# Where the column sums' products stand, and when an image's last output is finished: a fused attention kernel in fp32 pieces

## The chip, the cores and the metric

The kernel runs on one core of a Trainium2 chip. The metric is the device time of one execution in microseconds; the time before is a median of three runs, 2464.89 us (2459.27 to 2466.72). All profile lines are from one profiled execution.

## The reference, cut to what matters

```python
q = einsum('bwhc,cd->bwhd', x, Wq) + bq      # x: 4 images, 64 x 64 x 256
k = einsum('bwhc,cd->bwhd', x, Wk) + bk      # 128 channels
v = einsum('bwhc,cd->bwhd', x, Wv) + bv      # 256 channels
pq, pk, pv = (t.reshape(B, -1, 4096) for t in (q, k, v))
energy = einsum('bcn,bcm->bnm', pq, pk)      # 4096 x 4096 for each image
attention = softmax(energy, axis=-1)
out = einsum('bcm,bnm->bcn', pv, attention)
return gamma * out.reshape(x.shape) + x
```

For each image it is an attention over 4096 positions with 128 channels for q and k and 256 for v. The softmax is not shifted by its maximum on the main path: the kernel takes the exponential directly, sums it over m, and divides at the end.

## The kernel before, in words

**Stages.** The four images (`b`) run one after the other, and the order of every instruction on every engine is written out by hand. Each image has two stages.

*Projection*, 16 steps `i`. A step transposes an x tile on TensorE (`xt`, L123), copies it out of PSUM on ScalarE (`xts`, L129), and multiplies for q and k (`qk`, L136) and for v (`v`, L157). VectorE and ScalarE split q and k into fp32r pieces `f` (L259, L261), and POOL's queue stores these in DRAM (`kf`, L264; `qd`, L266). The x tiles are loaded by SP's queue (L82) into three buffers, so a load waits until the transposes of three tiles before are done. v is split into `vh`, `vl`, `vd` (L279, L283); the last two v tiles are split later, in units 2 and 6 of the attention.

*Attention*, 128 units `u` of 256 rows of m each. Sixteen units make a group `g` of 512 columns n; an image has eight groups. A unit does, in this order on TensorE: two "cross" products for the unit three ahead (L308), the first half's six products (`attend(b, u, 0)`, L365: two with `vh` and two with `vl` into bank a0, two with `vd` into b0), four energy products for the unit two ahead (L323), and the second half's six products (a1, b1). ScalarE scales the cross products in place (L309), takes the exponentials (L326) and their upper pieces `h` (L332). VectorE adds the exponentials into the running sum `s` (L341) and makes the lower pieces `ld` (L346, L348). POOL's queue loads k (L296), three units ahead of their use in the energies, and q (L290).

**PSUM.** Four banks (`ps_e`) hold energies, and four (`ps_o`) hold the results of a group: a0, b0, a1, b1. A tile that takes a bank waits until the bank's former tile has been read. At the end of a group `emptied` (L379) reads a0 and b0 after the first half of unit 15, and a1 and b1 after its second half, all on ScalarE.

**The finish of a group.** In unit 15 the running sum is split into two pieces `zf` (L388, L390). `finish` is a generator: `start` runs it up to its first `yield`, and each `proceed` runs it one `yield` on. Its pieces are:

1. two products of ones with the pieces of the sum (`z`, L400, in a bank of `ps_o`) and a copy of one row of the result by ScalarE (L401);
2. the store of that row in DRAM (`zd`, L403, SP);
3. its load, spread over partitions (`rall`, L405, SP);
4. the reciprocal (L407) and the addition of the a and b parts of the output (L408), on VectorE;
5. the store of the reciprocals (`rd`, L410, SP);
6. their load, broadcast to all partitions (`r`, L413, SP);
7. after one empty piece, the multiplication of the output by r (L416, VectorE);
8. the load of x that adds to the output in SBUF (L420, POOL's queue);
9. after one empty piece, the store of the output (L423, SP).

`proceed` is called once in each unit that doesn't end a group. It is also called in every projection step, and once between images. So an image's last group, started at the end of unit 127, is finished in the projection of the next image. Between images TensorE does the z products, the transposes of the next image's second tile (`transposed(1)`) and the qk products of its first (`project_qk(b + 1, 0)`). The last group of the last image has a path of its own, `finish_last`.

SP's and POOL's queues issue their transfers in the order of the program: a transfer that waits for its data holds those behind it.

Of the kernel before, what the change touches and what calls it, by code (L numbers as in the profile page):

```python
# [9 lines left out]
F32 = mybir.dt.float32  # L10
# [10 lines left out]
def kernel(  # L21
# [36 lines left out]
    nc = tc.nc  # L58
    B, W, H, C = x.shape
    P = 128  # L60
# [26 lines left out]
    ones_r = const.tile([P, P], F32R, name="ones")  # L87
# [86 lines left out]
    NB = 512  # L174
    NJ = NB // P
    NG = N // NB
# [22 lines left out]
    with ExitStack() as fast:  # L199
# [10 lines left out]
        ps_o = pool("ps_o", 1, space=PSUM)  # L210
# [9 lines left out]
        images, qd, kf, units, loads, now = [], {}, {}, {}, {}, {}  # L220
# [9 lines left out]
        def proceed():  # L230
            for pieces in list(active):
                if next(pieces, StopIteration) is StopIteration:
                    active.remove(pieces)
# [20 lines left out]
        def project_qk(b, i):  # L254
            images[b].qk(i)
            qk = now["qk"]
            f = ppool.tile([P, 2, 2, 3, P], F32R, tag="ld", name=f"f_{b}_{i}")
            h = f[:, :, :, 0, :]
            nc.scalar.activation(h, qk, AF.Identity, scale=UPPER / 64)  # L259
            for j, s, op in ((1, -64.0, ALU.add), (2, 64.0 * (1.0 + E), ALU.subtract)):  # L260
                nc.vector.scalar_tensor_tensor(  # L261
                    f[:, :, :, j, :], h.bitcast(F32), s, qk, ALU.mult, op
                )
            nc.gpsimd.dma_start(kf[b, i], f[:, 1])  # L264
            for s in range(2):
                nc.gpsimd.dma_start(qd[b, i // NJ + NG // 2 * s][:, i % NJ], f[:, 0, s])  # L266
# [21 lines left out]
        def load_q(b, g):  # L288
            t = work.tile([P, NJ, 3, P], F32R, tag="q", name=f"q_{b}_{g}")
            nc.gpsimd.dma_start(t, qd[b, g])  # L290
            loads[b, "q", g] = t
# [7 lines left out]
        def forms(b, u, i, f):  # L299
            return loads[b, "k", u][:, i, f, :], loads[b, "q", u // NU][:, :, f, :]  # L300
# [10 lines left out]
        def energy(b, u):  # L311

            if u >= STEPS:
                return
            if u % NU:
                x = ppool.tile([P, 2, NB], F32, tag="x", name=f"x_{b}_{u}", bufs=3)
            else:
                x = ppool.tile([P, 2, NB], F32, tag="s", name=f"s_{b}_{u // NU}")
            units[b, u] = x
            for i in range(2):  # L320
                e = units.pop((b, "e", u, i))
                for f in range(2):
                    nc.tensor.matmul(  # L323
                        e, *forms(b, u, i, f), start=False, stop=(f == 1), skip_group_check=True
                    )
                nc.scalar.activation(x[:, i, :], e, AF.Exp, scale=(1.0 + E) / E)  # L326
# [47 lines left out]
        def emptied(b, g, j):  # L374

            if j == 0:
                now["o"] = work.tile([P, 2, 2, NB], F32, tag="o", name=f"o_{b}_{g}", bufs=1)
            for c, scale in enumerate((gam1, gam)):
                nc.scalar.activation(  # L379
                    now["o"][:, c, j, :], now["ab"[c], j], AF.Identity, scale=scale  # L380
                )

        def sum_forms(b, g):
# [6 lines left out]
            nc.vector.tensor_tensor(l, s[:, 0, :], h.bitcast(F32), ALU.subtract)  # L390
            yield

        def finish(b, g, o, s):
            n = b * NG + g
            r4 = rall[:, n, :]
            row = lambda t: t[n : n + 1, :]
            spread = lambda t: row(t).rearrange("o (p j) -> (o p) j", j=NJ)
            zp = ps_o.tile([P, NB], F32, tag="b0", name=f"z_{b}_{g}")
            for f, x in enumerate(now["z"]):
                nc.tensor.matmul(zp, ones_r, x, start=(f == 0), stop=(f == 1))  # L400
            nc.scalar.copy(s[0:1, 0, :], zp[0:1, :])  # L401
            yield
            nc.sync.dma_start(row(zd), s[0:1, 0, :])  # L403
            yield
            nc.sync.dma_start(r4, spread(zd))  # L405
            yield
            nc.vector.reciprocal(r4, r4)  # L407
            nc.vector.tensor_tensor(o[:, 0], o[:, 0], o[:, 1], ALU.add)  # L408
            yield
            nc.sync.dma_start(spread(rd), r4)  # L410
            yield
            r = work.tile([P, NB], F32, tag="r", name=f"r_{b}_{g}", bufs=1)
            nc.sync.dma_start(r, rd[n, :].partition_broadcast(P))  # L413
            yield
            yield
            nc.vector.tensor_tensor(  # L416
                o[:, 0], o[:, 0], r.unsqueeze(1).to_broadcast([P, 2, NB]), ALU.mult
            )
            yield
            nc.gpsimd.dma_start(o[:, 0], xg[b, g], accum_op=ALU.add)  # L420
            yield
            yield
            nc.sync.dma_start(og[b, g], o[:, 0])  # L423
# [49 lines left out]
        def begin(b, i):  # L473

            if i in (4, 5, 6, 7):
                load_k(b, i - 4)
            if i == 6:
                load_q(b, 0)
            if i in (11, 13):
                energy(b, (i - 11) // 2)  # L480
            if i in (10, 11, 13):
                cross(b, (i - 9) // 2)
            if i == 12:
                load_k(b, 4)
            if i in (12, 14):
                upper(b, i // 2 - 6)

        image(0)
        for b in range(B):
            pr = images[b]  # L490
            if b == 0:
                now["banks"] = energies
                pr.transposed(0)

                wp = ps_o.tile([P, P], F32, tag="b1", name="wp1")
                for _ in range(2):
                    nc.tensor.matmul(wp, ones, ones, start=True, stop=True)
                pr.transposed(1)
                project_qk(b, 0)
            for i in range(1, NI):  # L500
                if i == 3:
                    now["banks"] = outputs
                if i + 1 < NI:
                    pr.transposed(i + 1)
                begin(b, i)
                project_qk(b, i)
                if i == NI - 1:
                    halves(b, 0)
                project_v(b, i - 1)
                proceed()  # L510
            project_v(b, NI - 1)
            for u in range(STEPS):
                g, t = divmod(u, NU)
                final = (b, u) == (B - 1, STEPS - 1)
                if t == 6 and g + 1 < NG:
                    load_q(b, g + 1)
                if u == STEPS - NU and b + 1 < B:
                    image(b + 1)
                if u >= STEPS - 3 and b + 1 < B:
                    now["banks"] = energies  # L520
                    if u == STEPS - 3:
                        images[b + 1].load(0)
                    elif u == STEPS - 2:
                        images[b + 1].transposed(0)
                if (b, u) == (B - 1, STEPS - 6):
                    xr = ppool.tile([P, 2, NB], F32, tag="s", name="xr")
                    nc.sync.dma_start(xr, xg[b, g])

                beside = iter(())
                if u in (2, 6):  # L530
                    beside = halve_v(b, NI - 2 + u // 4)
                cross(b, u + LOOK + 1)
                if t == NU - 1 and not final:
                    total = now["sum"]
                    for _ in sum_forms(b, g):
                        pass
                if not final:
                    attend(b, u, 0)
                    if t == NU - 1:
                        emptied(b, g, 0)  # L540
                energy(b, u + LOOK)
                next(beside, None)
                upper(b, u + LOOK)
                load_k(b, u + LOOK + 3)
                halves(b, u + 1)
                next(beside, None)
                if final:
                    finish_last(b, u, xr)
                    break
                attend(b, u, 1)  # L550
                if t == NU - 1:
                    emptied(b, g, 1)
                    start(finish(b, g, now["o"], total))
                else:
                    proceed()
            if b + 1 < B:
                images[b + 1].transposed(1)
                project_qk(b + 1, 0)
                proceed()

    NB = 512
    NG = N // NB
    NJ = NB // P
    NP = NM // 2
    with tc.If(nc.values_load(again[0:1, 0:1]) > 0), ExitStack() as general:
# [7 lines left out]
        ps_o = pool("go", 1, space=PSUM)  # L573
        for b in range(B):
# [16 lines left out]
            for g in range(NG):  # L591
                ps = []
                mx = work.tile([P, 2, NB], F32, tag="mx", name=f"gmx_{b}_{g}")
                for t in range(NP):
                    sp = ps_s.tile([P, 2, NB], F32, tag="s", name=f"gs_{b}_{g}_{t}")
                    for h in range(2):
# [4 lines left out]
                            start=True,  # L601
                            stop=True,
# [31 lines left out]
                for t, p in enumerate(ps):  # L634
# [8 lines left out]
                    for h in range(2):  # L643
                        for s in range(2):
# [4 lines left out]
                                start=(t == h == 0),  # L649
                                stop=(2 * t + h == NM - 1),  # L650
# [43 lines left out]
```

## Time and profile before

| what | before |
|---|---|
| median of three runs | 2464.89 us (2459.27 to 2466.72) |
| the profiled execution | 2466.14 us, span 2464.4 us |
| granted TensorE clock, mean of the span | 0.991 |
| busy TensorE / VectorE / ScalarE | 97% / 84% / 75% |
| SP waits for the copy of z (L403 <- L401) | 1231.0 us, 31 times |
| SP waits for the accumulating load (L423) | 639.4 us, 31 times |
| mean DMA rate | 137 GB/s |

A row of the timeline gives the start in us, the duration in us, the engine, the line, the operation, what it writes and reads, the sizes, the count of merged instructions, and in brackets how long the engine stood idle before it and what ended that. PE is TensorE, DVE VectorE, ACT ScalarE; a q behind an engine's name stands for its queue. A row of the waits gives the waiting engine and line, what ended the wait, and then the total in us, the number of times and the longest. A row of windows gives the two ends and the width, the busy time of PE, PEld (weight loads), DVE, ACT and POOL with their counts, the granted clock, the DMA engines' busy share and GB/s. A row of DMA issues gives the count, the size of each and the median time from issue to landing in us. TensorE's products are pipelined: one of 512 columns is shown with 0.39 us, but the next starts 0.23 us after it.

### The profile page before, as it was taken

To read this page: it belongs to the slowest core of one execution; us is meant where nothing else is said; L and a number is where in the kernel's file an instruction comes from. 1 tells how busy PE (TensorE), PEld (TensorE's weight loads), DVE (VectorE), ACT (ScalarE), POOL (GpSimd) and SP (SyncE) were. 2 spreads that over 40 slices of the span, in tenths; PEclk is the share of its full clock that TensorE was granted. 3 is DMA by queue.
4 is the path that set the end of the run, shared out by engine and by line. 5 is a ranking of instruction groups with operands and counts; after the bars stand their busy time and mean duration, and the time that the engine had idled before them with its cause. 6 is when DMAs were issued, how large, how long until landed. Compare 5 with 4: busy or idle time off the path is not lost.

```text
span 2464.4 us, 30518 instructions
## 1 busy us (share of the span) xinstructions
PE 2391.0 (97%) x10588; PEld 1973.5 (80%) x10588; DVE 2072.6 (84%) x2058; ACT 1856.3 (75%) x3071; POOL 429.3 (17%) x781
## 2 busy tenths in 40 slices
PE   9999999999899999999989999999998999999998
PEld 7888888888788888888867888888887788888886
DVE  5888888888688888888868888888886988888887
ACT  5777777787577877877757777777875787787775
POOL 4211111110321111111032111111113111111110
PEclk9999999999999999999999999999999999999999
DMA  8544444444854444444484444444449444444443
GB/s 257 155 122 118 129 113 127 129 127 101 258 148 129 114 125 126 121 122 131 105 258 146 125 122 122 123 119 122 129 110 269 135 130 125 122 122 125 117 121 90
DMA packets 155215, 338.22 MB, mean 137 GB/s; under 512 B 23471, under 2 KB 56751, under 8 KB 155054
## 3 DMA queue, kind: packets, MB, share of 16 engines
q0 software_dynamic: 114656, 293.52, 44.0%
q1 hardware_dynamic: 39854, 42.41, 5.7%
q8 instruction: 87, 1.43, 0.2%
q14 instruction: 74, 0.61, 0.1%
q10 hardware_dynamic: 544, 0.26, 0.0%
HBM read 268.89 MB, written 67.24 MB: 136 GB/s over the span
## 4 chain that ended last, share of the span: by engine, by line
PE 80%; ACT 11%; DMA 4%; DVE 2%; issue 1%; POOL 0%; SPq 0%; ACTq 0%; DVEq 0%; POOLq 0%
PE a L365 33%; PE b L365 18%; PE e L323 17%; PE e L308 8%; DMA qd<-f 3%; ACT o L379 3%; ACT h L332 2%; PE qk L136 2%; ACT s L326 1%; ACT x L326 1%; PE v L157 1%; DMA x<-in_x_dram 1%; ACT e L309 1%; ACT v L166 1%; ACT f L259 1%
## 5 line engine op out<-in xcount | busy, mean ns | idle before, releaser
L326 ACT ACTIVATE x<-e 128x512 f32<-128x512 f32 x960 | 522.3, 597 | 408.9 <-PE e L323 408.9
L341 DVE TENSOR_TENSOR s<-s,x 128x1024 f32<-128x1024 f32 x480 | 587.8, 1225 | 182.7 <-ACT x L326 174.1
L365 PE MATMUL b<-ld,vd 128*128 128x512 f32 x2048 | 634.6, 391 | 27.1 <-ACT s L401 24.4
L365 PE MATMUL a<-ld,vl 128*128 128x512 f32 x2048 | 631.8, 390 | 3.9 <-DVE ld L346 3.9
L365 PE MATMUL a<-h,vh 128*128 128x512 f32 x2048 | 632.1, 390 | 0.5 <-ACT v L166 0.5
L346 DVE TENSOR_TENSOR ld<-x,h 128x1024 fp32r<-128x1024 f32 x480 | 585.4, 1220 | 3.9 <-DMA qd<-f 3.9
L348 DVE SCALAR_TENSOR_TENSOR ld<-h,x 128x1024 fp32r<-128x1024 f32 x480 | 585.2, 1219 | 0.0
L296 POOL DMA_DIRECT2D k<-kf x512 | 272.4, 532 | 1702.4 <-PE e L323 1569.2
L323 PE MATMUL e<-q,k 128*128 128x512 f32 x2048 | 551.5, 391 | 0.0
L309 ACT ACTIVATE e<-e 128x512 f32<-128x512 f32 x1024 | 543.9, 564 | 0.0
L332 ACT ACTIVATE h<-x 128x1024 fp32r<-128x1024 f32 x480 | 509.6, 1062 | 14.9
L365 PEld LDWEIGHTS b<-ld,vd 128*128 128x128 f32 x2048 | 381.5, 188 | 119.6 <-ACT s L401 36.6
L365 PEld LDWEIGHTS a<-ld,vl 128*128 128x128 f32 x2048 | 384.4, 188 | 85.6 <-DVE ld L346 5.6
L323 PEld LDWEIGHTS e<-q,k 128*128 128x128 f32 x2048 | 385.4, 189 | 80.4
L365 PEld LDWEIGHTS a<-h,vh 128*128 128x128 f32 x2048 | 384.2, 188 | 81.8 <-ACT v L166 1.0
L308 PE MATMUL e<-q,k 128*128 128x512 f32 x1024 | 318.0, 392 | 0.0
L308 PEld LDWEIGHTS e<-q,k 128*128 128x128 f32 x1024 | 192.8, 189 | 40.0
L261 DVE SCALAR_TENSOR_TENSOR f<-f,qks 128x512 fp32r<-128x512 f32 x128 | 82.8, 689 | 60.4 <-ACT f L259 60.4
L136 PE MATMUL qk<-wqk_sb,xts 128*128 128x256 f32 x512 | 127.2, 393 | 0.6 <-ACT xts L129 0.5
L259 ACT ACTIVATE f<-qks 128x512 fp32r<-128x512 f32 x64 | 40.4, 630 | 110.6 <-DVE qks L145 73.8
L157 PE MATMUL v<-xts,wv_sb 128*128 128x256 f32 x512 | 121.7, 382 | 1.2 <-DVE qks L145 1.2
L157 PEld LDWEIGHTS v<-xts,wv_sb 128*128 128x128 f32 x512 | 98.3, 192 | 15.7 <-PE qk L136 2.0
(68 smaller groups left out, 1044.8 us busy)
## 6 DMA issues: line engine op xcount, KB each, us to landing
k<-kf POOLq DMA_DIRECT2D x512, 384.0 KB, 3.4
kf<-f POOLq DMA_DIRECT2D x64, 384.0 KB, 3.3
qd<-f POOLq DMA_DIRECT2D x128, 192.0 KB, 3.6
q<-qd POOLq DMA_DIRECT2D x32, 768.0 KB, 5.0
x<-in_x_dram SPq DMA_DIRECT2D x64, 256.0 KB, 5.3
o<-in_x_dram POOLq DMA_DIRECT2D x31, 512.0 KB, 5.9
out_dram<-o SPq DMA_DIRECT2D x31, 512.0 KB, 3.6
r<-rd SPq DMA_DIRECT2D x31, 256.0 KB, 4.1
```

The source lines that it names most:

```text
L136: nc.tensor.matmul(qk[:, s, :], self.xt[i][:, k, s, :], wqk_sb[:, k, :], start=(k == 0), stop=(k == KC - 1),)
L157: nc.tensor.matmul(vp[:, eh, :], wv_sb[:, k, eh * P : (eh + 1) * P], self.xt[i][:, k].rearrange("p s a -> p (s a)"), start=(k == 0), stop= ...
L296: nc.gpsimd.dma_start(t, kf[b, u % NU])
L308: nc.tensor.matmul(e, *forms(b, u, i, 2), start=True, stop=False, skip_group_check=True)
L309: nc.scalar.mul(e, e, -1.0 / (1.0 + E))
L323: nc.tensor.matmul(e, *forms(b, u, i, f), start=False, stop=(f == 1), skip_group_check=True)
L326: nc.scalar.activation(x[:, i, :], e, AF.Exp, scale=(1.0 + E) / E)
L332: nc.scalar.activation(h, units[b, u], AF.Identity, scale=UPPER)
L341: nc.vector.tensor_tensor(s, s, x, ALU.add)
L346: nc.vector.tensor_tensor(l, x, h.bitcast(F32), ALU.subtract)
L348: nc.vector.scalar_tensor_tensor(d, h.bitcast(F32), 1.0 + E, x, ALU.mult, ALU.subtract)
L365: nc.tensor.matmul(to, (vh, vl, vd)[f][:, t + NU * i, j * P : (j + 1) * P], units[b, u][f][:, i, :], start=(t == 0 and i == 0 and f != 1), ...
```

## The change

The z products and the copy leave `finish` and become a function of their own, `sums`. z takes bank b1 in place of b0. Inside an image `sums` is called for group g - 1 in unit 0 of group g, behind the first half's products and ahead of the energies. At an image's end it is called between the transposes and the qk products of the next image. The two other calls of `proceed`, in the projection's steps and between images, are gone, so the finish of an image's last group goes on in units 0 to 9 of the next image's first group. `start` now runs `finish` up to a `yield` ahead of the store of zd.

```diff
+        def sums(b, g, s):
+            zp = ps_o.tile([P, NB], F32, tag="b1", name=f"z_{b}_{g}")
+            for f, x in enumerate(now["z"]):
+                nc.tensor.matmul(zp, ones_r, x, start=(f == 0), stop=(f == 1))
+            nc.scalar.copy(s[0:1, 0, :], zp[0:1, :])
+
         def finish(b, g, o, s):
...
-            zp = ps_o.tile([P, NB], F32, tag="b0", name=f"z_{b}_{g}")
-            for f, x in enumerate(now["z"]):
-                nc.tensor.matmul(zp, ones_r, x, start=(f == 0), stop=(f == 1))
-            nc.scalar.copy(s[0:1, 0, :], zp[0:1, :])
             yield
             nc.sync.dma_start(row(zd), s[0:1, 0, :])
...
                 project_v(b, i - 1)
-                proceed()
             project_v(b, NI - 1)
...
                     attend(b, u, 0)
                     if t == NU - 1:
                         emptied(b, g, 0)
+                    elif t == 0 and g:
+                        sums(b, g - 1, total)
                 energy(b, u + LOOK)
...
             if b + 1 < B:
                 images[b + 1].transposed(1)
+                sums(b, NG - 1, total)
                 project_qk(b + 1, 0)
-                proceed()
```

## The prediction

> **What bounds the kernel now.** I read the page first, then TensorE's waits, then the timeline at the places where they lie.
>
> ```profile
> span 2464.4 us, 30518 instructions
> PE 2391.0 (97%) x10588; PEld 1973.5 (80%) x10588; DVE 2072.6 (84%) x2058; ACT 1856.3 (75%) x3071; POOL 429.3 (17%) x781
> ```
>
> TensorE sets the time: all other engines have room, so a microsecond counts where TensorE stands still. Its waits (total, times, longest):
>
> ```profile
> PE b L365 <- ACT s L401: 24.4, 28, 0.9
> PE xt L123 <- DMA x<-in_x_dram: 21.7, 8, 7.2
> ```
>
> Both belong to the change. The first comes at each of the 28 passages from one group to the next inside an image (4 images, 8 groups, 7 passages each); the second lies in the projections. A passage in the timeline:
>
> ```profile
> 145.65 1.22 DVE L348 SCALAR_TENSOR_TENSOR ld<-h,s 128x1024 fp32r<-128x1024 f32 x1
> 145.87 0.62 PE L400 MATMUL z<-zf,ones 128*128 128x512 f32 x2
> 147.26 0.62 PE L365 MATMUL a<-ld,vl 128*128 128x512 f32 x2
> 147.57 0.68 ACT L379 ACTIVATE o<-b,gam 128x512 f32<-128x512 f32 x1
> 148.14 0.56 ACT L401 COPY s<-z 1x512 f32<-1x512 f32 x1
> 148.61 1.04 ACT L309 ACTIVATE e<-e 128x512 f32<-128x512 f32 x2
> 148.75 0.72 PE L365 MATMUL b<-ld,vd 128*128 128x512 f32 x2 [0.87 <-ACT s L401]
> 149.99 1.09 ACT L326 ACTIVATE x<-e 128x512 f32<-128x512 f32 x2 [0.33 <-PE e L323]
> ```
>
> z takes bank b0. The next group's b products need b0 and wait until the copy of z is done, and the copy stands on ACT behind the emptying of a1 and b1. From 145.87 to 147.26 TensorE issues six products, 0.23 us apart; with the two at 147.26 the ninth slot is 147.72. It starts at 148.75, so a passage loses 1.03 us.
>
> The projections, by the v products of images 0, 1, 2 and 3 (min/median/max ns, first and last start):
>
> ```profile
> L157 PE MATMUL v<-xts,wv_sb x128: 379/379/634, 12.6 to 77.7; 128*128 128x256 f32 x128
> ```
> ```profile
> L157 PE MATMUL v<-xts,wv_sb x128: 379/379/631, 616.6 to 691.8; 128*128 128x256 f32 x128
> ```
> ```profile
> L157 PE MATMUL v<-xts,wv_sb x128: 379/379/454, 1230.7 to 1306.0; 128*128 128x256 f32 x128
> ```
> ```profile
> L157 PE MATMUL v<-xts,wv_sb x128: 379/379/379, 1844.9 to 1916.9; 128*128 128x256 f32 x128
> ```
>
> The same 128 products take 65.1 us in image 0 and 75.2, 75.3 and 72.0 us after it. Image 0 has no earlier group to finish, and the one wait of its projection is not for x:
>
> ```profile
> PE xt L123 <- ACT v L166: 1.9, 1, 1.9
> ```
>
> What the finish does to image 1:
>
> ```profile
> 659.80 0.59 SPq L423 DMA_DIRECT2D out_dram<-o  x1
> 660.48 7.48 SPq L82 DMA_DIRECT2D x<-in_x_dram  x4
> 666.30 1.09 PE L123 MATMUL xt<-ident,x 128*128 128x128 f32 x4 [5.67 <-DMA x<-in_x_dram]
> 669.75 2.45 PE L136 MATMUL qk<-wqk_sb,xts 128*128 128x256 f32 x8
> ```
>
> SP issues in program order. The store L423 waits for the accumulating load to land, and the next x loads stand behind it: they go out at 660.48, and TensorE idles 5.67 us until 666.30. The load of r (L413, which waits for rd) stands ahead of x loads in the same way. Behind the long wait eight qk products take 2.45 us; elsewhere 1.89 (row at 612.70 below).
>
> **The change, part by part.**
>
> *z in the next group's first unit, in b1 (28 times).* No instruction is added; two products and a copy move. From 145.87 on TensorE now does the two crosses, four a and two b products, with z ninth. The b products come up at 147.26 instead of 147.72; their ld is ready at 145.65 + 1.22 = 146.87, 0.39 us earlier, so no new wait. z needs b1, whose emptying ends at 147.57 + 0.68 = 148.25; with the 0.05 us that lie between the copy's end (148.70) and the product it released (148.75), z starts at 148.30. The wait does not vanish, it changes its owner and shrinks from 1.03 to 0.58 us: 0.45 us a passage, **12.6 us** in all. Behind the waiting z on TensorE stand four energy products and then the second half's a and b. The scalings L309 move ahead of the copy, so they start 0.47 us sooner; the copy follows at about 149.1, ends at 149.7, and the second half's b products come up at 148.30 + 10 x 0.23 = 150.6, 0.9 us later: covered. The exponentials start at about 149.7 instead of 149.99. Bounds: no gain, if the copy slips behind both exponentials (1.09 us against that 0.9); 1.03 us each (28.8 us) if b1 were free in time.
>
> *No proceed in the projections (3 images).* The zd, rall, rd, r and out transfers leave SP's queue ahead of the x loads; the accumulating load leaves POOL's queue between the stores of kf and qd; a reciprocal, an addition and a multiplication leave VectorE. What is then left is what image 0 has, so I take its 65.1 us: 10.1 + 10.2 + 6.9 = **27.2 us**. It isn't the floor: image 0 itself waits 1.9 us for ACT and slows behind it. Bounds: below, that only the bytes matter:
>
> ```profile
> o<-in_x_dram POOLq DMA_DIRECT2D x31, 512.0 KB, 5.9
> out_dram<-o SPq DMA_DIRECT2D x31, 512.0 KB, 3.6
> r<-rd SPq DMA_DIRECT2D x31, 256.0 KB, 4.1
> ```
> ```profile
> 616.50:692.00 75.50, 65.48 (x309) 55.90 (x308) 50.35 (x93) 42.79 (x85) 28.10 (x52) 0.93 0.83 250
> 147.00:214.00 67.00, 66.13 (x292) 54.37 (x291) 58.23 (x53) 53.09 (x88) 10.17 (x18) 1.00 0.48 126
> ```
>
> 1.25 MB at the 250 GB/s of image 1's window are 5.2 us an image, 16 in all. Above, TensorE's own work: busy 65.48 us in that window, partly at a clock of 0.93, so about 60.9 at full clock; 4.2 below image 0's 65.1, so 12.6 more over three images, 39.8 in all.
>
> The clock shows in these windows as 0.93 with the long waits and 1.00 across the 1 us waits of the passages. The Trainium skill (TensorE: Matmul & The Clock Gate, "HAM oscillation — how this bites in real kernels") says that gaps over some 3.4 us drop the array to half its clock until it has been busy again. The trace agrees as far as the 2.45 against 1.89 us go. By that rule at most 1.7 us a long gap would come back, which image 0's time already counts.
>
> *z at an image's end (3 images).* It now stands behind the four transposes and ahead of qk:
>
> ```profile
> 611.79 0.63 PE L400 MATMUL z<-zf,ones 128*128 128x512 f32 x2
> 612.12 0.68 ACT L379 ACTIVATE o<-b,gam 128x512 f32<-128x512 f32 x1
> ...
> 612.26 0.60 PE L123 MATMUL xt<-ident,x 128*128 128x128 f32 x4
> ...
> 612.70 1.89 PE L136 MATMUL qk<-wqk_sb,xts 128*128 128x256 f32 x8
> ```
>
> The transposes now start at 611.79 and end issuing at 612.23; z waits for b1 until 612.80 + 0.05 and takes 0.46, so qk starts at 613.31, not 612.70: 0.6 us an image, **1.8 us lost** (0, if a later wait swallows it).
>
> *The finish in the next image's first group (3 images).* Group 0 also splits the last two v tiles on VectorE in units 2 and 6, the very units in which the finish adds and multiplies. Group 0 of image 1, then the finish in group 1:
>
> ```profile
> 710.43 1.22 DVE L348 SCALAR_TENSOR_TENSOR ld<-h,x 128x1024 fp32r<-128x1024 f32 x1
> 712.37 0.62 PE L365 MATMUL b<-ld,vd 128*128 128x512 f32 x2
> 723.27 0.69 DVE L283 SCALAR_TENSOR_TENSOR vl<-vh,v 128x512 fp32r<-128x512 f32 x1 [1.10 <-ACT vh L279]
> 726.75 1.22 DVE L348 SCALAR_TENSOR_TENSOR ld<-h,x 128x1024 fp32r<-128x1024 f32 x1
> 728.69 0.62 PE L365 MATMUL b<-ld,vd 128*128 128x512 f32 x2
> ```
> ```profile
> 763.97 0.34 SPq L405 DMA_DIRECT2D rall<-zd  x1
> ```
> ```profile
> 772.71 0.17 DVE L407 RECIPROCAL rall<-rall 128x4 f32<-128x4 f32 x1
> 773.91 1.22 DVE L341 TENSOR_TENSOR s<-s,x 128x1024 f32<-128x1024 f32 x1
> ...
> 789.03 1.22 DVE L416 TENSOR_TENSOR o<-o,r 128x1024 f32<-128x1024 f32 x1
> 790.16 1.22 DVE L341 TENSOR_TENSOR s<-s,x 128x1024 f32<-128x1024 f32 x1
> ```
>
> Reciprocal and addition hold VectorE 773.91 - 772.71 = 1.20 us, the multiplication 1.13. The tile ready at 711.65 is needed at 712.37: 0.72 spare, so 0.48 late. In unit 6 VectorE first waits 1.10 us for ACT, which absorbs the older delay; then 727.97 + 1.13 against 728.69 is 0.41 late. Together 0.9 us an image, **2.7 us lost** (bounds 0 and 2.33 us an image). The SP and POOL issues cost nothing here: SP has no x loads then, and POOL's k loads run three units ahead, as in 28 other groups. The images' outputs come later, but the last image's end is untouched.
>
> Sum: -12.6 - 27.2 + 1.8 + 2.7 = -35.3 us. The profiled execution took 2466.14 us (1.7 outside its span), so 2430.8; the median shown is 2464.89, and on it the forecast is **2429.6 us**.
>
> **The rivals.**
>
> *Bytes, not order.* The Trainium skill (DMA: Bandwidth & Descriptors, "Issuing engines are not separate DMA queues") says that transfers of all issuing engines share the same 16 DMA engines and interleave, which speaks against gaining much by reordering queues. As a mechanism here: the x loads are late for want of bandwidth, and the projections gain only the 16 us above: 2464.89 - 24 = 2441. For it: the DMA share of 0.83 in the window above. Against it: image 0 loads and stores the same x, qd and kf without a wait for x, and the x loads of 660.48 weren't even issued before.
>
> *Projections near TensorE's floor.* The relief also ends the ACT waits: 39.8 us, 2417. Against it: image 0 has them without any finish.
>
> *The passage keeps its wait.* The copy slips behind the exponentials, or z's wait is as long as the old one: 12.6 us fewer, 2442. For it: only 0.39 and 0.9 us of margin.
>
> *Slower.* VectorE, in order, is held at the reciprocal in group 0 because the zd and rall transfers queue behind the projection's last stores. In group 1 the reciprocal runs 8.7 us after rall's issue at 763.97, so it costs from a return over 8.7 us on. To eat the whole gain it must hold TensorE another 38 / 3 = 12.7 us an image; at 17 us an image the time would be 2478. Against it: even r, of 256 KB, lands in 4.1 us.
>
> **How the numbers follow.** Forecast 0.66; bytes 0.12; floor 0.08; passage 0.09; slower mechanism 0.05, of which 0.03 end beyond 0.3% and 0.02 within it. A measurement of this kernel tells 0.3% (7.4 us) from no change. So faster 0.94, same 0.03 (0.01 for two shortfalls at once), slower 0.03. The range, 2416 to 2444, reaches to the floor, bytes and passage cases.
>
> **What would show it.** A wait of z for ACT o, 28 times, about 0.4 us as the page counts it, in place of 24.4 us; passages 0.45 us nearer; the v rows of images 1 to 3 at about 65 us, with no SP store between x loads and almost no xt wait for x; in group 0 of images 1 to 3 two new short waits for ld L348. I am wrong if the v rows stay above 70 us, or if the wait at z is 1 us.

## The result, and the profile after

The changed kernel takes 2434.12 us in the median of four runs (2433.08 to 2438.69), beside 2463.74 us for the kernel before: a ratio of 0.9885, 95% interval 0.9865 to 0.9905. That is 29.6 us less where 35.3 were forecast, and inside the range. The profiled execution took 2433.35 us, 32.8 less than that of before. The page's first lines:

```profile
span 2431.6 us, 30522 instructions
PE 2385.8 (98%) x10588; PEld 1963.4 (81%) x10588; DVE 2071.1 (85%) x2058; ACT 1851.9 (76%) x3071; POOL 429.2 (18%) x781
```

TensorE's waits (total, times, longest):

```profile
PE z L396 <- ACT o L379: 11.8, 31, 0.5
PE xt L123 <- ACT v L166: 8.4, 4, 2.9
...
PE a L365 <- DVE ld L346: 4.8, 4, 1.8
PE b L365 <- DVE ld L348: 4.1, 12, 0.5
```

The wait of b for the copy (24.4 us) is gone, and so is that of xt for x (21.7 us). z has a wait of its own, for ScalarE's emptying of b1. In the projections xt now waits for ScalarE. The first passage in the timeline, and the z of the next one:

```profile
147.03 0.62 PE L365 MATMUL b<-ld,vd 128*128 128x512 f32 x2
147.28 0.68 ACT L379 ACTIVATE o<-b,gam 128x512 f32<-128x512 f32 x1
147.84 1.08 ACT L309 ACTIVATE e<-e 128x512 f32<-128x512 f32 x2
148.01 0.73 PE L396 MATMUL z<-zf,ones 128*128 128x512 f32 x2 [0.36 <-ACT o L379]
148.57 1.09 PE L323 MATMUL e<-q,k 128*128 128x512 f32 x4
148.83 0.58 ACT L397 COPY s<-z 1x512 f32<-1x512 f32 x1
149.31 1.06 ACT L326 ACTIVATE x<-e 128x512 f32<-128x512 f32 x2
...
150.40 0.62 PE L365 MATMUL b<-ld,vd 128*128 128x512 f32 x2
...
214.48 0.73 PE L396 MATMUL z<-zf,ones 128*128 128x512 f32 x2 [0.38 <-ACT o L379]
```

z's slot is 147.03 + 0.46 = 147.49. ScalarE frees b1 at 147.28 + 0.68 = 147.96, and z starts at 148.01, 0.52 us late. From one z to the next it is 214.48 - 148.01 = 66.47 us. Before, it was from 145.87 to this:

```profile
212.83 0.62 PE L400 MATMUL z<-zf,ones 128*128 128x512 f32 x2
```

That is 66.96 us: a group with its passage is 0.49 us shorter. The v products of images 1, 2 and 3 after the change:

```profile
L157 PE MATMUL v<-xts,wv_sb x128: 379/379/379, 1218.5 to 1283.0; 128*128 128x256 f32 x128
```
```profile
L157 PE MATMUL v<-xts,wv_sb x128: 379/379/631, 613.7 to 680.9; 128*128 128x256 f32 x128
...
L157 PE MATMUL v<-xts,wv_sb x128: 379/379/379, 1820.5 to 1886.6; 128*128 128x256 f32 x128
```

In image 1 they span 67.2 us, in image 2 (the row that stands alone) 64.5, in image 3 66.1; before 75.2, 75.3 and 72.0. In image 1 SP now issues its x loads with nothing between them, and stores zd only behind the last of them, at 658.81; but ScalarE waits:

```profile
640.48 18.28 SPq L82 DMA_DIRECT2D x<-in_x_dram  x4
...
649.80 0.63 ACT L259 ACTIVATE f<-qks 128x512 fp32r<-128x512 f32 x1 [5.11 <-DMA qd<-f]
651.21 0.66 PE L123 MATMUL xt<-ident,x 128*128 128x128 f32 x4 [2.75 <-ACT v L166]
652.34 3.26 PE L136 MATMUL qk<-wqk_sb,xts 128*128 128x256 f32 x8
...
658.81 0.46 SPq L405 DMA_DIRECT2D zd<-s  x1
```

The next tile of f needs a buffer whose stores to qd haven't landed; ScalarE, in order, holds the evacuation of v behind it, and TensorE stops. It is the kind of wait that image 0 had before.

The two profiled executions, cut at the starts of named TensorE products:

| stretch | before, us | after, us | difference |
|---|---|---|---|
| last b product of an image to the next image's first v, three times | 15.1 | 17.3 | +2.2 |
| v products, images 1 to 3 | 222.4 | 197.7 | -24.7 |
| first group, images 1 to 3 | 204.7 | 207.3 | +2.6 |
| groups 1 to 7 of all images | 1859.4 | 1847.7 | -11.7 |
| image 0 up to its group 1 | 146.1 | 145.4 | -0.7 |
| what is left | 16.6 | 16.2 | -0.4 |

The z of the passage out of group 0 (0.46 us) stood in the first group's stretch before and stands in the next now. With that put right, 28 passages gained 13.5 us, 0.48 each, and the first groups of images 1 to 3 lost 3.9 us, not 2.6.

The windows of the v products after the change, of image 1 and then of image 2:

```profile
613.50:681.00 67.50, 64.12 (x309) 54.53 (x307) 47.86 (x89) 42.22 (x85) 26.89 (x51) 0.97 0.86 256
1218.50:1283.50 65.00, 62.57 (x309) 53.24 (x307) 47.92 (x90) 42.05 (x85) 26.93 (x51) 1.00 0.89 268
```

Before, image 1's window was 75.50 us with TensorE busy for 65.48, at a clock of 0.93. So of its 8.0 us, 6.6 are idle time that is gone, and 1.4 are products, which run at a lower clock for less of the time.

### The profile page after: what moved, and what is told of

Same layout as the page of the kernel before. It is cut to its first block, busy times and chain, and to the rows that moved or that the text cites. A ratio compares the mean times of both kernels' runs of the same rounds, so it can differ in the third digit from the quotient of the medians.

```text
span 2431.6 us, 30522 instructions
## 1 busy us (share of the span) xinstructions
PE 2385.8 (98%) x10588; PEld 1963.4 (81%) x10588; DVE 2071.1 (85%) x2058; ACT 1851.9 (76%) x3071; POOL 429.2 (18%) x781
## 4 chain that ended last, share of the span: by engine, by line
PE 80%; ACT 11%; DMA 4%; DVE 2%; issue 2%; POOL 0%; ACTq 0%; DVEq 0%; POOLq 0%
PE a L365 34%; PE e L323 17%; PE b L365 17%; PE e L308 8%; DMA qd<-f 4%; ACT o L379 3%; ACT h L332 2%; ACT s L326 1%; PE qk L136 1%; ACT x L326 1%; PE z L396 1%; PE v L157 1%; ACT v L166 1%; ACT f L259 1%; ACT e L309 1%
## 5 line engine op out<-in xcount | busy, mean ns | idle before, releaser
L136 PEld LDWEIGHTS qk<-wqk_sb,xts 128*128 128x128 f32 x512 | 95.0, 193 | 17.7 <-ACT xts L129 5.2
```

The lines of the kernel that those rows point to most:

```text
L136: nc.tensor.matmul(qk[:, s, :], self.xt[i][:, k, s, :], wqk_sb[:, k, :], start=(k == 0), stop=(k == KC - 1),)
```

## The experiments

Times are medians, beside runs of the kernel before on the same chip. "v products" are the spans of images 1, 2 and 3 from the first to the last start. A single execution differs from the median by up to 7 us, so the terms are read from the traces.

**One half each.** First, only the z of the passages moves; an image's last group keeps the old course:

```diff
 # against the changed kernel
         def finish(b, g, o, s):
+            if g == NG - 1:
+                zp = ps_o.tile([P, NB], F32, tag="b0", ...)   # products and copy as before
...
                 project_v(b, i - 1)
+                proceed()
...
-                sums(b, NG - 1, total)
                 project_qk(b + 1, 0)
+                proceed()
```

> Only the z products inside an image move (unit 0 of the next group, bank b1); an image's last group keeps its z in b0 and its finish in the next projection. Theory (the passage and the projection are separate terms): the 28 passages lose 0.5 us instead of 1.0 and nothing else changes, about -13.4 us against before, some 2450; the v products of images 1 to 3 stay at 72 to 75 us. Rival (the terms hang together, the gain in the passages being a shift of VectorE's or ScalarE's lateness): passages gain less than 8 us here, or the projections move too.

Measured: 2449.32 us beside 2464.48, ratio 0.9936 (0.992 to 0.9953): 15.2 us less by the medians, 15.8 by the ratio. Its waits:

```profile
PE xt L123 <- DMA x<-in_x_dram: 25.7, 10, 6.5
PE z L396 <- ACT o L379: 10.4, 28, 0.4
```

The passages are those of the changed kernel. The v products stay at 73.9, 75.6 and 74.5 us. So the passages' gain stands by itself.

Second, only the two calls of `proceed` go:

```diff
 # against the kernel before
                 project_v(b, i - 1)
-                proceed()
...
                 project_qk(b + 1, 0)
-                proceed()
```

> Only the finish of an image's last group waits for the next attention; z stays in b0 in its old place. Theory: v products of images 1 to 3 at 64 to 67 us as in the changed kernel (together about 25 us less than before), 0.9 us an image lost in group 0, passages at 1.0 us as before: about -22 us, some 2442. Rival (the projections gained from the new place of z as well): v products stay above 70 us in at least one image.

Measured: 2445.34 us beside 2464.48, ratio 0.9915 (0.9899 to 0.993): 19.1 us less by the medians, 21 by the ratio.

```profile
PE b L365 <- ACT s L401: 24.4, 28, 0.9
PE xt L123 <- ACT v L166: 11.9, 4, 4.7
PE a L365 <- DVE ld L346: 7.6, 4, 4.0
...
PE xt L123 <- DMA x<-in_x_dram: 0.8, 1, 0.8
```

The wait for x is gone but for 0.8 us, and the v products take 69.6, 64.5 and 64.4 us, while the passages' 24.4 us stand as before. The first product that needs a lower piece in a first group waits longer here, up to 4.0 us, and that in image 0, which the edit doesn't touch.

**Order or bytes.** In the kernel before, ScalarE's queue issues the x loads of images 1 to 3, a step further ahead; the finish stays in the projection with all its bytes:

```diff
 # against the kernel before
-                self.xs[g] = load_x(self.xpool, self.b, g)
+                self.xs[g] = load_x(self.xpool, self.b, g, nc.scalar if self.b and g > 2 else nc.sync)
...
-            for g in range(i, i + 2):
+            for g in range(i, i + (3 if self.b else 2)):
                 self.load(g)
```

> The kernel before, but the x loads of images 1 to 3 from the fourth on are issued by ScalarE's queue, one step further ahead, so that they no longer stand behind the finish on SP. The finish with all its bytes stays in the projection, on SP. Theory (order, not bytes): the waits of xt for x go from 21.7 us to under 4, v products at 65 to 69 us, 2440 to 2450 (ScalarE pays about 0.5 us a step for the issues, which it can hide). Rival (bytes: the x loads are late for want of bandwidth): the waits for x or for stores stay at 15 us or more, v products above 71 us, 2458 or more.

Measured: 2451.58 us beside 2464.48, ratio 0.9944 (0.993 to 0.9959), just above the span that the order theory gave.

```profile
PE xt L123 <- DMA x<-in_x_dram: 11.9, 7, 3.3
```
```profile
L157 PE MATMUL v<-xts,wv_sb x128: 379/379/631, 618.3 to 687.4; 128*128 128x256 f32 x128
```

The v products (the row is image 1's) take 69.1, 66.7 and 67.3 us, together 19.4 less than before with the same bytes. The waits for x fell by half, not to under 4 us. VectorE's and POOL's part of the finish stays in the projection here too. So the x loads' way past the finish gives 19.4 of the 24.7 us; this run doesn't part the other queue from the step further ahead.

The other way round: the changed kernel with transfers of the finish's sizes put back into the projections, waiting for nothing and read by nobody (the accumulating load as a plain one):

```diff
 # against the changed kernel; extra(b, i) in steps 4, 7 and 9 of images 1 to 3
+            if i == 4:
+                nc.sync.dma_start(to[:, 0], rd[b * NG - 2, :].partition_broadcast(P))
+            elif i == 7:
+                nc.gpsimd.dma_start(to, xg[b - 1, NG - 1])
+            else:
+                nc.sync.dma_start(scratch[:, 0], wqk_sb)
+                nc.sync.dma_start(scratch[:, 1], wv_sb)
```

> The changed kernel with transfers of the same sizes put back into the projections of images 1 to 3, on the same queues but waiting for nothing: a 256 KB broadcast and two stores of 256 KB on SP, an x load of 512 KB on POOL. Nothing reads what they bring. Theory (order): the v products grow by at most 5 us an image, most likely 1 to 3; 2437 to 2445. Rival (bytes): they go back to 72 to 75 us, 2455 or more.

Measured: 2441.27 us beside 2464.48, ratio 0.9903 (0.9889 to 0.9918); the v products take 68.4, 68.0 and 66.6 us, 5.2 more than in the changed kernel's profile in all. The two experiments agree: with the finish's bytes but without its waits the three spans take 203.0 and 202.9 us together, beside 222.4 before, and this one loads x no further ahead than before. So order gives about 19 us. The bytes' part, some 5 us, is less sure: the eight profiled executions here with the changed kernel's projection, whatever their other edits, take 194.2 to 201.9 us, 197.3 in the mean.

**The changed kernel again, and its weak places.** The next four ran on one chip, beside 2464.4 us.

```diff
 # no edit: the changed kernel once more
```

> The changed kernel once more, so that the next versions stand beside it on the same chip. Theory: its profile repeats (31 waits of z for ScalarE, 11 to 12 us; v products of images 1 to 3 within 64 to 69 us), 2430 to 2438. If the difference to before is nearer to 36 us than to 28, the sum of the two halves (15 and 21 us by their own runs) holds, and the first measurement lay at the low end of its interval; if it is 28 us again, the halves don't add up and something of one takes away from the other.

Measured: 2436.9 us, ratio 0.9887 (0.9872 to 0.9902). It repeats the first result. By the medians the halves (15.2 and 19.1 us, each with an interval of some 4 us to either side) sum to 34.3 us, and neither has z at an image's end, which costs 2.2; so 32.1 stand beside 27.5 here and 29.6 in the first measurement. The intervals meet, and the difference isn't settled. By the terms of the traces the halves do add up: 13.4 us in the passages of the first half and 23.8 in the v products of the second, where the changed kernel had 13.5 and 24.7. This execution shows where time can be lost again; in image 3 its first group begins so:

```profile
1890.88 0.73 PE L365 MATMUL a<-ld,vl 128*128 128x512 f32 x2 [2.06 <-DVE ld L346]
...
1892.65 1.82 PE L323 MATMUL e<-q,k 128*128 128x512 f32 x4
```

The v products took 66.0, 64.2 and 64.0 us, 28.2 less than before, but the first groups of images 1 to 3 lost 7.2 us (counted as above), 3.3 more than in the first profile. VectorE's first lower piece needs one of the two buffers that the last f tiles had, and waits for their stores. But this is not what the change lost: that wait is the same in both profiles of the changed kernel and in that of before:

```profile
DVE ld L346 <- DMA qd<-f: 5.3, 8, 1.0
```

The 3.3 us lie in the first two units of images 2 and 3 (1.2 and 2.0 us). There TensorE ran at a clock of 0.50 from 1288.6 to 1292.0 and from 1892.7 to 1896.2, as the row at 1892.65 shows, and in image 3 the first wait was 0.8 us longer (2.06 for 1.26). In the first profile neither happened.

Emptying b1 ahead of a1 at a group's end:

```diff
 # against the changed kernel, in emptied
-            for c, scale in enumerate((gam1, gam)):
+            for c, scale in ((0, gam1), (1, gam)) if j == 0 else ((1, gam), (0, gam1)):
```

> The changed kernel with one edit: at a group's end ScalarE empties b1 ahead of a1. Theory (z waits only because b1 is emptied last): b1 is free 0.57 us sooner, the wait of z goes from 11.8 us to under 2, a passage from 0.5 us to 0.1 or less, 12 to 16 us faster than the changed kernel, 2418 to 2424. Rival (ScalarE as a whole sets the passage: the scalings, the copy and the exponentials come no sooner, and TensorE waits for them a few products later): the same total moves to waits of e for the scalings or exponentials, and less than 6 us is gained.

Measured: 2420.65 us (2415.91 to 2422.44), ratio 0.9815 (0.98 to 0.9829), 16.2 us less than the changed kernel; in the traces the groups 1 to 7 of all images are 14.1 us shorter.

```profile
146.37 0.67 ACT L379 ACTIVATE o<-b,gam 128x512 f32<-128x512 f32 x1
146.69 0.63 PE L365 MATMUL b<-ld,vd 128*128 128x512 f32 x2
146.94 0.68 ACT L379 ACTIVATE o<-a,gam 128x512 f32<-128x512 f32 x1
147.16 0.68 PE L396 MATMUL z<-zf,ones 128*128 128x512 f32 x2
```
```profile
PE z L396 <- ACT o L379: 1.0, 3, 0.3
```

b1 is free at 147.04, z follows its b products 0.47 us behind, and no wait of e takes its place (0.4 us in all). The three waits left are those at the images' ends. The rival, that ScalarE as a whole sets the passage, falls.

The finish one unit later in the first group:

```diff
 # against the changed kernel
-                else:
+                elif u != 1:
                     proceed()
```

> The changed kernel with one edit: unit 1 of an image's first group calls no proceed, so the finish adds and multiplies in units 3 and 7, not in 2 and 6, where VectorE splits the last v tiles. Theory (the two meet on VectorE): the waits of the b products in units 4 and 8 of group 0 (0.5 us each, three images) go, 2 to 3 us faster than the changed kernel. Rival (VectorE is short of time in group 0 wherever the finish stands): they come one unit later, and nothing is gained.

Measured: 2430.99 us (2429.04 to 2431.98), ratio 0.9861 (0.9846 to 0.9877), 5.9 us less than the changed kernel beside it.

```profile
PE b L365 <- DVE ld L348: 1.9, 4, 0.5
```

The waits of b for ld fall from 12 in the first profile, or 10 in the second, to 4, which is about 2 us as the page counts. Counted from unit to unit it is more: units 4 and 8 took 4.7 us where the others take 4.08, and now no unit behind the first two takes more than 4.15. That gives 3.7 us over three images. A further 2.0 us lie in the first two units, where the second profile had its low clock twice; that part is not the edit's. The collision on VectorE is shown; its rival falls.

The copy of z behind both exponentials, the prediction's rival for the passage:

```diff
 # against the changed kernel: sums returns the copy, which is called behind energy(b, u + LOOK)
-                        sums(b, g - 1, total)
+                        late = sums(b, g - 1, total)
                 energy(b, u + LOOK)
+                if t == 0 and g:
+                    late()
```

> The changed kernel with the copy of z behind the two exponentials on ScalarE in the 28 passages, the case named as a rival in the prediction. Theory (the margin of the copy is a little under an exponential pair): the second half's b products wait about 0.4 us for the copy in each passage, so a passage loses 0.9 us in place of 0.5, 8 to 14 us slower than the changed kernel. Rival (the copy has room): no wait, no difference.

Measured: 2450.49 us, ratio 0.9939 (0.9926 to 0.9953), 13.6 us more than the changed kernel.

```profile
PE z L396 <- ACT o L379: 11.6, 31, 0.5
...
PE b L365 <- ACT s L397: 7.1, 28, 0.3
```

The second half's b products wait 28 times for the copy, as the margin said. The groups 1 to 7 take 15.5 us more over 28 passages, 0.55 each, where 0.4 was expected. The first of these products comes 0.42 us late; and the two of them then take 0.56 us in place of 0.46, as they also do behind other waits (z above, from 148.01 to 148.57). That rival would have taken the passages' gain, and no more.

**Better versions.** Both edits together:

```diff
 # against the changed kernel: the edits of the b1 version and of the later finish
```

> The changed kernel with b1 emptied ahead of a1 and with the finish one unit later in group 0. Theory (two separate waits): the gains add, 16 us and 3 to 6 us, 2414 to 2419. Rival (a shorter passage leaves VectorE less time in group 0): no better than b1 first alone, 2420 or more.

Measured: 2416.38 us (2413.25 to 2422.76) beside 2464.97, ratio 0.9798 (0.9782 to 0.9814): faster than both kernels, in the expected span, but not told from the b1 version alone by its interval.

```diff
 # against the version with both edits
-                images[b + 1].transposed(1)
-                sums(b, NG - 1, total)
+                sums(b, NG - 1, total, "b0")
+                images[b + 1].transposed(1)
```

> The version before this one, and at an image's end z stands ahead of the transposes in bank b0 again, as in the kernel before. Theory (with b1 emptied first, z at an image's end costs its own place and about 0.6 us of wait): the way from the last attention product to the first v product goes from 5.6 back to 5.0 us in images 1 to 3, 1.5 to 2 us less in all, at the border of what is measured. Rival (a later wait of the projection takes it): the way is shorter and the projection longer by the same.

Measured: 2413.66 us (2413.13 to 2415.67), ratio 0.9793 (0.9778 to 0.9808). From an image's last b product to the next first v it is 5.03 us again, 5.63 with z behind the transposes. The time isn't told from the version before it.

```diff
 # against the version with both edits
-            if i in (4, 5, 6, 7):
-                load_k(b, i - 4)
-            if i == 6:
+            if i in (4, 7, 9, 11):
+                load_k(b, (4, 7, 9, 11).index(i))
+            if i == 5:
                 load_q(b, 0)
```

> The version with both edits, and the loads of the first k and q tiles spread over the projection's steps 4, 5, 7, 9 and 11 in place of 4 to 7. Theory (what is left of the projections' waits is the stores of f that stand behind the 768 KB of q and the k loads on one queue): the v products of all four images fall to 61 to 63 us from 64 to 68, 8 to 14 us faster. Rival (the DMA engines are full in the projection, whatever the order): the waits move to later steps, the v products stay at 64 to 68 us, or the first unit of group 0 waits longer.

Measured: 2414.95 us, ratio 0.9788 (0.9772 to 0.9805): no difference. The v products stay at 65.9, 67.5 and 63.9 us, and xt waits as long for ScalarE:

```profile
PE xt L123 <- ACT v L166: 7.9, 5, 2.8
```

The theory that q and k loads on the same queue hold the stores falls; why the stores of f land late in some steps stays open.

## Why the prediction was right, point by point

- *Passages, 12.6 us.* Right: 13.5 us in the profile, 0.48 against 0.45 a passage; z waits 0.52 us where 0.58 were worked out. That the wait would only change its owner is what the trace shows, and the b1 version shows the owner: ScalarE's order at the group's end. The margins named held: the copy ends at 148.83 + 0.58 = 149.41, 1.0 us ahead of the b product at 150.40.
- *Projections, 27.2 us.* Right in mechanism and size: 24.7 and 28.2 us in two profiles. Image 0 as the measure held, with what it contains: its own span was 63.7 to 67.1 us over the executions here. The rival "bytes, not order" was wrong as the main cause, since order brings about 19 us with the bytes still there; some 5 us are left for the bytes, where the step gave them 16. "Near TensorE's floor" didn't come: once x is on time, f's stores hold TensorE. The floor was also put too low: TensorE's own work was 62.57 us at a clock of 1.00 (image 2), not 60.9. The step scaled all busy time by 0.93, but that is a mean over the window, idle time included: in image 1 the clock was 0.50 from 664.1 to 670.8, and TensorE was busy for 4.50 of the 6.70 us. ScalarE's waits for the stores grew:

```profile
ACT f L259 <- DMA qd<-f: 42.4, 14, 5.2
```

  They were 36.8 us before.
- *z at an image's end, 1.8 us lost.* Right: 2.2 us.
- *The finish in the first group, 2.7 us lost.* The place was right, the size too small. The two waits came in the units named, in image 1 here:

```profile
701.06 0.61 PE L365 MATMUL a<-ld,vl 128*128 128x512 f32 x2
702.04 0.73 PE L365 MATMUL b<-ld,vd 128*128 128x512 f32 x2 [0.37 <-DVE ld L348]
702.61 0.63 PE L323 MATMUL e<-q,k 128*128 128x512 f32 x2
...
718.06 0.63 PE L365 MATMUL a<-ld,vl 128*128 128x512 f32 x2
718.97 0.73 PE L365 MATMUL b<-ld,vd 128*128 128x512 f32 x2 [0.29 <-DVE ld L348]
719.55 1.07 PE L323 MATMUL e<-q,k 128*128 128x512 f32 x4
```

  The b products come up at 701.52 and 718.52 and start 0.52 and 0.45 us late, near the 0.48 and 0.41 that were worked out. What the step left out is that the two products behind such a wait take 0.57 us in place of 0.46. From unit to unit the two meetings cost 1.27 us an image, 3.8 in all, nearly all of the 3.9 us that the first groups lost in this profile. The 7.2 us of the second profile hold 3.3 more, mostly from the low clock named above, which the step didn't count. Image 0, which has the free projection in every kernel, shows such a spread too (68.0 to 73.0 us for its first group).
- *The sum.* The two profiled executions differ by 32.8 us, for 35.3. The projections gave 2.5 us less, the first groups cost 1.2 more and z at an image's end 0.4 more, the passages gave 0.9 more; the rest is image 0 and the ends. By the medians it is 29.6 us, since the profiled execution of before lay 2.4 us above its runs' median (2466.14 against 2463.74) and that of after 0.8 below. The second measurement has 27.5 us.
- *Slower.* The reciprocal was never held: in image 1 it ran straight behind the v tiles of unit 2, with no idle time. SP issued zd at 658.81 and rall at 661.31, behind its last x load and still in the projection.

```profile
696.70 0.68 DVE L283 SCALAR_TENSOR_TENSOR vd<-vh,v 128x512 fp32r<-128x512 f32 x1
697.30 0.17 DVE L409 RECIPROCAL rall<-rall 128x4 f32<-128x4 f32 x1
```

## What to carry to other kernels

A transfer that waits for data holds everything behind it on its queue, so a store of old results belongs behind the loads of the next stage, or on another queue; what it costs is best read from a stage that runs without it, as image 0 did here. When a product is moved off a bank that is read late, look at which bank it moves to and when that one is emptied: turning the order of two evacuations round was worth as much as the move itself. Work that is moved out of a stage should be laid against what its new place already does in the same units.

## What the runs showed of the hardware that was not expected

The clock fell after shorter gaps than the long waits of before. After a wait of 2.75 us eight qk products took 3.26 us (row at 652.34), and after one of 2.06 us four energy products took 1.82 us (row at 1892.65) instead of 1.09, while the passages' waits of 0.4 to 0.9 us slowed nothing that followed. In image 2 of the second profile only three waits of 0.52, 0.48 and 0.50 us, within 3 us, came ahead of a clock of 0.50 (the last three figures of the row are the clock, the DMA share and GB/s):

```profile
1288.60:1291.90 3.30, 3.30 (x8) 2.57 (x9) 2.37 (x3) 1.18 (x2) 0.33 (x1) 0.50 0.81 210
```

In the first profile the same three waits (0.53, 0.47 and 0.49 us) were followed by a clock of 1.00. So the length of a single gap does not tell here whether the clock falls. The Trainium skill (TensorE: Matmul & The Clock Gate, "HAM oscillation — how this bites in real kernels") gives some 3.4 us as the gap to stay below; here it dropped after shorter ones, and the measurement decides.
